# Bias sums of a projection moved from TensorE to VectorE, and one projection step written ahead of other work

## The chip, the cores and the metric

The kernel runs on one core of one Trainium2 chip. The metric is device time in microseconds (us), the median over several runs. The core has five engines that work side by side, each through its own queue: PE (matrix products, with a separate row PEld for the loads of their stationary operand), DVE (elementwise operations and reductions), ACT (activation functions and copies), POOL (here mostly issuing transfers) and SP (issuing transfers). PE writes its products to PSUM, in banks that the other engines read out.

## The reference, cut to what matters

Four images of 32 x 32 positions with 768 channels go through two layers, each of them `x = x + attention(group_norm(x))` with 12 heads of 64 channels. Layer 1 forms its q, k and v with a depthwise 3 x 3 convolution and a layer norm, and has a projection at the end:

```python
v = layer_norm(dwconv3x3(v, w_pool_v), g_v, b_v)
...
attn = softmax(qf * scale @ kf.T + rel_h + rel_w)
o = attn @ vf + ori_q
return o @ w_proj.T + b_proj
```

The layer norm of v ends with an added bias `b_v` of 64 numbers, the same for all heads. The rows of a softmax sum to one, so this bias goes through the attention unchanged and can be left out there; what it adds to the projection is one number for each output channel, `w_proj` times `b_v` repeated over the heads. The kernel works it out once, in `pbias`, together with `b_proj`.

## The kernel before, in words

Channels lie on the 128 partitions, six groups of 128 (`NC`), and the 1024 positions of an image along the free dimension, in two halves of 512 (`HALF`). A **stage** is one image in one layer; there are eight, in the order (0,0), (1,0), (0,1), (1,1), (2,0), (3,0), (2,1), (3,1) (image, layer), numbered from 0. A stage has six **items**, each a pair of heads, and the attention of an item takes 16 **steps**.

*The order of the work.* `attend` yields after each step. It writes the scores of four key tiles (L794, L796: PE) with their exponentials (L801: ACT), two steps later the four products with v (L818), and so on. A list `events` holds, for each step, the pieces of other work that are written at that point: the preparation of the next items (`Pair.plan`), group norms, and the projection of the stage before. Within a step the pieces are written in the order in which they were added to the list. PE, DVE, ACT and POOL keep the order in which the program writes their instructions; each engine takes its own instructions in that order, and waits where one needs a result that isn't there.

*PSUM.* Of the four scores written together, the first and the last use the same pair of banks (`ps_a`), the second and the third use two others (`place_b`, `place_c`), which the other work also borrows. The fourth score thus needs the first one's exponential to be done, and the other work's next bank needs the second's.

*Preparing an item of layer 1.* In its 24 steps, from -8 to 15, q, k and v are formed in turn: a product (`padded`, L131, copied out on ACT, L519), nine taps of the convolution (`taps`: DVE, L534 and L536), centring (`centre`: transposes on PE, L548, and DVE, L551 and L552), squaring (`square`: ACT, L558), the sums of squares (`squares`: DVE, L562 and L563), and `norm`: Ln and Exp on ACT (L153, L155), four small DVE operations (L157 to L160), the scaling (L574) and for v a memset (L576). At step 15 come `squares` and `norm` of v, and two taps of the next item.

*The projection* (`project`) uses seven products instead of eight for each pair of output groups, three pairs in all. `four(pair)` makes four of them, `three(pair)` the other three; every product is `m`, which accumulates over three head pairs, six matmuls (L131). Before them `sums` forms sums and differences of the attention outputs on DVE (L876). `put` adds bias and residual on DVE (L890) and, where there is one, a further term (L892), and stores; `add` is L895. In `three`, the second accumulation into a bank has to wait until L895 has read the first. The stationary operands are read from HBM in tiles `wproj_t`, two buffers, by `load`. Where the next stage is in layer 1 (stages 1, 2, 5 and 6, called `late` in the code), the six parts come at steps 9, 9 (`four`), 11 (`three`), 13, 13, 15, 17, 17, 19 of that stage; so step 15 holds `three(1)`.

*The biases.* In stage 2 only, which is (0,1), `four` computes two columns of `pbias` in each of its three calls: with the second weights tile of the pair, six matmuls with one column (L911), three head pairs for each of two output groups, then an addition on DVE (L913).

## Time and profile before

| | |
|---|---|
| median of 3 runs | 3838.24 us (3836.82 to 3839.79) |
| the profiled execution | 3838.91 us, its span 3837.1 us |
| PE busy | 3769.4 us, 98% of the span |
| DVE busy | 2468.8 us, 64% |
| ACT busy | 1792.4 us, 47% |
| L911, bias matmuls | 36 records of 250 ns, from 1465.5 to 1545.5 us |
| L895 in `three`, what PE waits for it | 7.4 us in 8 waits |

The page of a profile shows one execution. Busy times are sums over an engine's instructions with overlaps taken out; a row of the timeline gives start, length, engine, line, operation, result and inputs, the number of instructions merged into it, and in brackets how long the engine was idle before and what ended that. A float32 matmul appears as two records. Products overlap on PE: the next row can begin before the one before it ends, so the cost of a group is read from its start to the start of the next.

### The profile page before, as it was taken

How to read it: one execution, taken by the hardware profiler on the slowest of the kernel's cores; microseconds unless marked ns; L12 is line 12 of the kernel's file. 1: busy time of each engine (PE TensorE's matmuls, PEld its weight loads, DVE VectorE, ACT ScalarE, POOL GpSimd, SP SyncE). 2: the span in 40 equal slices, each digit the busy share in tenths (PEclk: the TensorE clock that was granted, in tenths of full speed). 3: DMA queues.
4: the chain of work that ended last, by engine and by line, in shares of the span. 5: the costliest groups of instructions: out<-in, count | busy, mean ns of one | idle time of the engine just before them, and what ended most of it. 6: DMA issues, size and time to landing. Idle time of an engine off the chain costs nothing.

```text
span 3837.1 us, 76049 instructions
## 1 busy us (share of the span) xinstructions
PE 3769.4 (98%) x32988; PEld 1643.0 (43%) x32988; DVE 2468.8 (64%) x3068; ACT 1792.4 (47%) x2573; POOL 478.1 (12%) x870
## 2 busy tenths in 40 slices
PE   8999999999999999999999999999999999999998
PEld 3535535533344443344535445355343444434442
DVE  2566554559678777688454564455686877867774
ACT  2455434545345553455534554254442555534552
POOL 0111100111111111111200010011111111111120
PEclk9999999999999999999999999999999999999999
DMA  4344442331431223311333222522124222142123
GB/s 151 104 123 114 135 144 90 100 80 41 123 94 48 60 55 97 120 48 48 82 113 119 56 76 60 176 61 74 43 55 142 64 58 57 48 124 61 47 57 99
DMA packets 211013, 330.61 MB, mean 86 GB/s; under 512 B 47570, under 2 KB 100562, under 8 KB 210672
## 3 DMA queue, kind: packets, MB, share of 16 engines
q1 hardware_dynamic: 122912, 212.26, 17.8%
q0 software_dynamic: 87760, 113.40, 12.4%
q8 instruction: 263, 4.31, 0.5%
q14 instruction: 78, 0.64, 0.1%
HBM read 184.62 MB, written 40.10 MB: 59 GB/s over the span
## 4 chain that ended last, share of the span: by engine, by line
PE 88%; DVE 8%; ACT 2%; issue 1%; DMA 1%; SPq 0%; DVEq 0%; POOL 0%; ACTq 0%
PE qkv L131 19%; PE s L794 16%; PE av L818 15%; PE m4m L131 5%; PE m1m L131 4%; PE m3m L131 4%; PE s L796 4%; PE p3p L131 3%; PE p4p L131 3%; PE rel L605 3%; PE p1p L131 2%; PE m L131 2%; DVE shared L536 2%; PE ln_c L548 2%; PE z L763 1%
## 5 line engine op out<-in xcount | busy, mean ns | idle before, releaser
L801 ACT ACTIVATE e<-s 128x1024 f32<-128x1024 f32 x768 | 773.5, 1024 | 415.4 <-PE s L796 386.7
L794 PE MATMUL s<-q,k 64*128 64x512 f32 x3072 | 808.2, 603 | 12.1 <-ACT e L801 11.0
L131 PE MATMUL qkv<-xn,wqkv_t 128*64 128x512 f32 x3648 | 814.3, 595 | 2.6 <-DVE gmean L323 2.6
L536 DVE SCALAR_TENSOR_TENSOR shared<-shared,sm 128x1056 f32<-128x1056 f32 x576 | 758.1, 1316 | 15.6
L796 PE MATMUL s<-bias,ones 64*128 64x512 f32 x1536 | 611.0, 789 | 0.9 <-DMA bias<-whole 0.9
L818 PE MATMUL av<-e,vt 128*64 128x512 f32 x2624 | 595.6, 596 | 0.0
L632 POOL DMA_DIRECT2D bias<-high x384 | 205.6, 555 | 2187.7 <-ACT high L621 1950.8
L131 PEld LDWEIGHTS qkv<-xn,wqkv_t 128*64 128x64 f32 x3648 | 251.3, 137 | 490.5 <-issue 484.9
L812 DVE TENSOR_TENSOR acc<-acc,e 128x1024 f32<-128x1024 f32 x294 | 360.1, 1225 | 114.3 <-ACT e L801 87.4
L794 PEld LDWEIGHTS s<-q,k 64*128 64x128 f32 x3072 | 278.8, 186 | 271.6 <-issue 209.2
L519 ACT ACTIVATE shared<-qkv,sm 128x512 f32<-128x512 f32 (+1 forms) x288 | 129.3, 502 | 501.2 <-PE qkv L131 501.2
L818 PEld LDWEIGHTS av<-e,vt 128*64 128x64 f32 x2624 | 180.7, 137 | 350.5 <-issue 316.4
L796 PEld LDWEIGHTS s<-bias,ones 64*128 64x128 f32 x1536 | 148.5, 187 | 184.7 <-issue 182.9
L632 POOL DMA_DIRECT2D bias<-whole x384 | 207.2, 572 | 51.6 <-DVE whole L622 44.8
L810 DVE TENSOR_TENSOR acc<-e 128x1024 f32<-128x1024 f32 x49 | 60.0, 1225 | 214.6 <-ACT e L801 204.5
L731 ACT COPY weighed<-av 128x512 f32<-128x512 f32 x96 | 56.4, 587 | 278.5 <-PE av L818 264.9
L551 DVE TENSOR_REDUCE mean<-ln_c 128x8 f32<-128x512 f32 x144 | 98.5, 684 | 117.1 <-PE ln_c L548 117.1
L605 PEld LDWEIGHTS rel<-q,rel 64*32 64x32 f32 x6144 | 112.0, 106 | 78.3 <-issue 73.5
L737 POOL DMA_DIRECT2D z<-weighed x47 | 27.2, 579 | 885.7 <-ACT weighed L731 480.5
L562 DVE TENSOR_REDUCE lnv<-shared 128x16 f32<-128x1024 f32 x72 | 87.5, 1216 | 69.4 <-ACT shared L558 69.4
L605 PE MATMUL rel<-q_t,rel 64*32 64x32 f32 x6144 | 123.6, 195 | 2.2 <-issue 2.2
L605 PE MATMUL rel<-q,rel 64*32 64x32 f32 x6144 | 122.7, 195 | 1.8 <-issue 1.8
(158 smaller groups left out, 4398.8 us busy)
## 6 DMA issues: line engine op xcount, KB each, us to landing
bias<-high POOLq DMA_DIRECT2D x384, 128.0 KB, 2.9
bias<-whole POOLq DMA_DIRECT2D x384, 128.0 KB, 3.1
wqkv_t<-in_wqkv SPq DMA_DIRECT2D x78, 384.0 KB, 3.3
wqkv_t<-mixed SPq DMA_DIRECT2D x66, 384.0 KB, 3.1
wproj_t<-mixed SPq DMA_DIRECT2D x48, 384.0 KB, 3.3
wqkv_t<-in_wqkv SPq DMA_DIRECT2D x66, 192.0 KB, 2.5
xn<-in_x SPq DMA_DIRECT2D x24, 512.0 KB, 8.5
x<-in_x SPq DMA_DIRECT2D x48, 256.0 KB, 3.4
```

What stands on the lines that cost most here:

```text
L131: nc.tensor.matmul(ps[lo : lo + D], a[:, lo : lo + D], b, start=start, stop=stop, **kw)
L519: nc.scalar.activation(self.pad[s][:, rows, there : there + src.shape[2]], src, AF.Identity, bias=col(self.column(s)))
L536: nc.vector.scalar_tensor_tensor(y, window, tap, y, ALU.mult, ALU.add)
L551: nc.vector.tensor_reduce(of, heads, AX.X, ALU.add)
L562: nc.vector.tensor_reduce(v, squared.rearrange("p (a d) -> p a d", d=D), AX.X, ALU.add)
L605: nc.tensor.matmul(ps[lo : lo + S, k * S : (k + 1) * S].rearrange("p (b c) -> p b c", b=2), rel[rows, 2 * self.layer + i, first : first + ...
L632: nc.gpsimd.dma_start(sets, some.unsqueeze(1).to_broadcast([D // 2, 2, QC]))
L794: nc.tensor.matmul(ps[:, j, :], k[rows, keys], q[rows, cols], start=True, stop=False)
L796: nc.tensor.matmul(ps[:, j, :], ones[rows, keys], bias[c][rows, kt // 2, :], start=False, stop=True,)
L801: nc.scalar.activation(e, ps, AF.Exp)
L812: nc.vector.tensor_tensor(acc, acc, e, ALU.add)
L818: nc.tensor.matmul(av[j * D : (j + 1) * D, :], pair.vt[:, kt, j * D : (j + 1) * D], e[:, j, :], start=(kt == 0), stop=(kt == NKT - 1),)
```

## The change

The biases of layer 1's projection are summed over the three head pairs first: one reduction on DVE adds the three 128 x 128 weight blocks of each output group, into a free part of the tile that holds the attention sums (`extra(11)`), and PE multiplies the sums with the bias column, two matmuls where there were six.

Secondly `at` gets a flag `ahead`, with which a piece is put at the front of its step's list. It is set for the projection's part at step 15 of the `late` stages, so that `three(1)` is written before `squares`, `norm` and the taps of that step. This applies in four stages, the biases in one.

```diff
             if layer and b == 0:
 
                 ps = small_bank("pbias")
-                for i, at in ((0, 3), (1, 2)):
-                    for n in range(3):
-                        w_sum = weights[4 * pair + 1][:, 3 * (at % 2) + n, :]
-                        nc.tensor.matmul(ps[:, i : i + 1], w_sum, col(LN + 5), start=(n == 0), stop=(n == 2))
+                w_sum = extra(11)[:, : 2 * P].rearrange("p (a c) -> p a c", a=2)
+                both = weights[4 * pair + 1].rearrange("p (a n) c -> p a c n", n=3)
+                nc.vector.tensor_reduce(w_sum, both, AX.X, ALU.add)
+                for i in range(2):
+                    nc.tensor.matmul(ps[:, i : i + 1], w_sum[:, 1 - i, :], col(LN + 5), start=True, stop=True)
                 some = slice(2 * pair, 2 * pair + 2)
                 nc.vector.tensor_tensor(pbias[:, some], ps[:, 0:2], sm[:, BIAS[1] + 18 :][:, some], ALU.add)
...
-    def at(step, piece):
-        events.setdefault(step, []).append(piece)
+    def at(step, piece, ahead=False):
+        pieces = events.setdefault(step, [])
+        pieces.insert(0 if ahead else len(pieces), piece)
...
         for r, n in zip((9, 11, 13, 15, 17, 19) if late else (7, 9, 11, 13, 14, 15), (2, 1) * 3):
             for _ in range(n):
-                at(first + r, lambda products=products: next(products))
+
+                at(first + r, lambda products=products: next(products), late and r == 15)
```

## The prediction

> **What bounds the kernel now.** I read the page's first part, then the waits, then the timeline of the stretches that the change touches.

> ```profile
> span 3837.1 us, 76049 instructions
> PE 3769.4 (98%) x32988; PEld 1643.0 (43%) x32988; DVE 2468.8 (64%) x3068; ACT 1792.4 (47%) x2573; POOL 478.1 (12%) x870
> ```

> PE is busy 98% of the span, and the chain that ended last is 88% PE. So a microsecond of PE work removed, or of PE idling added, moves the end by about one; DVE time counts only where PE waits for it. The list of waits holds two rows that matter (total us, times, longest):

> ```profile
> PE s L794 <- ACT e L801: 11.0, 8, 1.8
> PE p1p L131 <- DVE os_sums L895: 7.4, 8, 1.6
> ```

> The second row is what the moved piece can save. The timeline shows it four times at 1.57 to 1.58 us (PE at 1030.7, 1534.2, 2927.6, 3427.9), always in `three(1)` of step 15; the other four are 0.27 us in `three(2)`, which the change leaves alone. The timeline of PE, then of DVE (start, length, engine, line, operation, count, idle before):

> ```profile
> 1529.90 2.75 PE L131 MATMUL p<-q,wproj_t 128*64 128x512 f32 x12
> 1534.22 2.80 PE L131 MATMUL p1p<-q,wproj_t 128*64 128x512 f32 x12 [1.58 <-DVE os_sums L895]
> ```

> ```profile
> 1524.22 1.22 DVE L562 TENSOR_REDUCE lnv<-shared 128x16 f32<-128x1024 f32 x1 [2.50 <-ACT shared L558]
> 1532.24 1.32 DVE L536 SCALAR_TENSOR_TENSOR shared<-shared,sm 128x1056 f32<-128x1056 f32 x1
> 1533.48 0.68 DVE L895 TENSOR_TENSOR os_sums<-os_sums,p1p 128x512 f32<-128x512 f32 x1
> ```

> The add L895, which lets PE accumulate further into the bank, stands behind squares, norm and two taps, while DVE also idled 2.5 and 3.14 us among them.

> The biases: PE first, then DVE, around the first and second of the three places.

> ```profile
> 1462.82 2.80 PE L131 MATMUL p4p<-os_sums,wproj_t 128*64 128x512 f32 x12
> 1465.54 1.50 PE L911 MATMUL pbias<-sm,wproj_t 128*128 128x1 f32 x12
> 1466.97 2.79 PE L131 MATMUL p3p<-os_sums,wproj_t 128*64 128x512 f32 x12
> ```

> ```profile
> 1463.60 2.67 DVE L536 SCALAR_TENSOR_TENSOR shared<-shared,sm 128x1056 f32<-128x1056 f32 x2
> 1466.18 1.89 DVE L876 TENSOR_TENSOR q<-q 128x512 f32<-128x512 f32 x3
> 1467.99 0.15 DVE L913 TENSOR_TENSOR pbias<-pbias,sm 128x2 f32<-128x2 f32 x1
> ...
> 1508.62 2.67 DVE L536 SCALAR_TENSOR_TENSOR shared<-shared,sm 128x1056 f32<-128x1056 f32 x2
> 1511.21 0.15 DVE L913 TENSOR_TENSOR pbias<-pbias,sm 128x2 f32<-128x2 f32 x1
> ```

> Today PE does not wait for DVE here: it has its sums at 1466.97, and DVE comes to the addition only at 1467.99. DVE is behind PE at the first two places.

> [...] L895 above waits its turn. [...] 512 elements take 0.684 us (L551) and 1024 take 1.216 (L562), 1.04 ns for each more. [...]

> **The change, part by part.**

> *Biases, PE work.* 12 passes take 1.43 us (1465.54 to 1466.97), 0.119 each. Two matmuls instead of six are 4 passes, 0.48 us: 0.95 saved, three times 2.85, if nothing waits.

> *Biases, the reduction.* It reads 768 elements: 0.684 + 256 x 1.04 ns = 0.95 us. Its innermost step is 128 floats[...]. Bound from above by the only strided pair at hand: ACT's permuted copy takes 1.281 us (L488) against 0.778 (L487) for 512 elements, 0.98 ns more each; 768 x 0.98 = 0.75, so 1.70. Below 0.95 the row of L551 gives no reason to go. I take 0.95 and keep 1.70 for the range.

> *Biases, the new wait.* The weight load of the bias matmul now needs the reduction, and everything on PE is queued behind it. After DVE's end PE starts some 0.06 us later (1533.48 + 0.68 to 1534.22), plus 0.19 for this weight load (L911's LDWEIGHTS)[...]: 0.25.
> - Pair 0: DVE reaches the reduction at 1467.99; end 1468.94; bias matmul 1469.19; p3p 1469.67 instead of 1466.97: **2.70 lost**.
> - Pair 1: DVE 1511.21, end 1512.16, matmul 1512.41, p3p 1512.89 instead of 1509.79: **3.10 lost**. DVE is fed by PE's work between the two places, so the second loss is not covered by the first.
> - Pair 2: worked out below, since the move decides it.

> The weights are no new DMA wait: the second tile of pair 2 is issued at 1537.06 and these loads take 3.3 us to land. `w_sum` lies in the last, unused twelfth of a tile that is held anyway.

> *The move.* `three(1)` issues 18 matmuls, five DVE operations, five weight and input loads and two stores. The pieces that it passes (squares, norm of V, two taps) have nothing on PE, SP or POOL, and on ACT only Ln and Exp, of which `three` has none. So PE, ACT, SP and POOL keep their order; only DVE's five operations go ahead of ten others. In stage (0, 1), times of before:
> - p1p's first product ends 1530.07; L895 follows at once, so p1p continues at 1529.90 + 2.57 = 1532.47: 1.75 earlier, the wait and its restart.
> - It ends 1535.22. DVE's put: L890 1535.29, L892 1536.08. The squares start only now, 1536.69, instead of 1524.22; L563 at 1537.94.
> - **What is late next:** Ln and Exp of this norm precede the four exponentials of the next scores in ACT's queue. Before they ran at 1528.3, ten us ahead of need. Now Ln runs at 1538.14. The first and fourth scores share one bank (`ps_a`), so the fourth waits for the first exponential.

> The trace has this chain already, eight times; one is:

> ```profile
> 1157.35 0.22 ACT L153 ACTIVATE ln_ln<-lnv 128x16 f32<-128x16 f32 x1 [2.74 <-DVE lnv L563]
> ...
> 1158.78 1.13 PE L794 MATMUL s<-q,k 64*128 64x512 f32 x4 [1.34 <-ACT e L801]
> ```

> From Ln to the fourth score 1.43 us, and 1.30 more to what follows. So the fourth score starts at 1539.57 and p4p at 1540.87 instead of 1541.50: **0.63 gained of 1.75**, in each of four stages. Bounds: 1.75 if ACT is not late; minus 0.3 if the chain is 0.9 us slower.

> *Pair 2.* DVE comes out later: Exp ends 1538.61, four small operations to 1539.47, norm to 1540.75, three taps to 1544.69 (before, DVE idled 5.99 us here). Reduction to 1545.64, matmul 1545.89, p3p 1546.37, instead of 1545.65: **0.72 lost**, and the 0.63 is contained in it. In the other three stages DVE is next wanted at 1546.2, so its lateness is covered by 1.5 us. V's norm, ready 1540.75, is first read by the product at 1553.4.

> **Sum.** 2.70 + 3.10 + 0.72 - 3 x 0.63 = **+4.6 us**. Against the profiled run's 3838.91 (span 3837.1 and 1.8 around it) 3843.5; that run lies 0.7 above the median of 3838.24, so the median becomes 3842.8, 0.12% more.

> **The rivals.**
> - *Nothing waits*: the move keeps its 1.75 four times and the biases their 2.85: -9.85, 3828.4. For it: the PE time is truly removed. Against: DVE's clock readings above, 2.5 and 2.9 us behind PE before the reduction is added. It also needs DVE's order to differ from the written one. 0.04.
> - *ACT's hold costs nothing*: the three other stages gain 1.75 each, pair 2 stays where DVE puts it: 6.5 - 5.25 = +1.3, 3839.5. Against: the eight waits on the exponential. 0.08.
> - *The strided reduction, slower than before by more than the bound*: the three reductions in stage (0, 1) are all on the path, so each us over 0.95 counts three times. At 1.70 the sum is +6.8 (3845.1), at 2.3 us, three times ACT's excess, +8.7 (3846.9). It passes the bound from 1.98 us. 0.18.
> - The forecast, with the reduction between 0.95 and 1.70: 0.70.

> **How the numbers follow.** A measurement of this kernel can tell about 0.2%, 7.7 us, from no change: 3830.6 to 3845.9. Forecast and second rival lie inside, the first below, the third above: faster 0.04, same 0.78, slower 0.18. The forecast's own range is 3841 to 3845.5. For 8 in 10 the range reaches down to 3838.5 (the second rival) and up to 3847.5 (the reduction at 2.3).

> **What would show it.** Right: PE waits for the reduction some 3.6, 4 and 2.3 us at the three bias matmuls; L895's four waits of 1.58 are gone; four waits of about 1.3 us of the fourth score on the exponential have come, PE's first list row going from 8 to 12 times. Wrong: no PE idling before the bias matmuls, a reduction far from 0.95, or exponentials that start with their scores after `three(1)`.

## The result, and the profile after

The changed kernel takes 3850.34 us (median of 7 runs, 3846.48 to 3851.88) against 3838.24 for the kernel before: a ratio of 1.0031, 95% interval 1.0022 to 1.0039. It is 12 us slower. The forecast was 4.6 us slower, with a range that ended at 3847.5.

The first part of the page of the changed kernel, for its profiled execution of 3850.34 us:

```profile
span 3848.5 us, 76002 instructions
PE 3771.7 (98%) x32964; PEld 1639.3 (43%) x32964; DVE 2472.7 (64%) x3071; ACT 1791.5 (47%) x2573; POOL 477.8 (12%) x870
```

PE has 24 records less, as the edit says, and yet 2.3 us more of busy time. Fewer instructions with more busy time is the first sign that some of them took longer than before. The list of PE's waits (total us, times, longest):

```profile
PE s L794 <- ACT e L801: 15.2, 13, 1.8
PE pbias L912 <- DVE os_sums L910: 9.4, 3, 3.9
...
PE p1p L131 <- DVE os_sums L895: 1.1, 4, 0.3
```

The waits moved as forecast. Of L895's eight waits the four long ones are gone; the exponential has five waits more, four of them of 0.86 us in the four late stages (the fifth, of 0.77 us at 1840.9, lies outside them); and a new row has come, the bias matmul (now L912) waiting for the reduction (L910) at all three places. The first place on the timeline, PE and DVE, and then from the kernel before the row of PE that follows its p3p:

```profile
1463.04 2.79 PE L131 MATMUL p4p<-os_sums,wproj_t 128*64 128x512 f32 x12
1469.26 0.61 PE L912 MATMUL pbias<-sm,os_sums 128*128 128x1 f32 x4 [3.43 <-DVE os_sums L910]
1469.80 4.49 PE L131 MATMUL p3p<-os_sums,wproj_t 128*64 128x512 f32 x12
1474.12 2.74 PE L131 MATMUL p4p<-q,wproj_t 128*64 128x512 f32 x12
```

```profile
1466.38 1.89 DVE L876 TENSOR_TENSOR q<-q 128x512 f32<-128x512 f32 x3
1468.18 1.03 DVE L910 TENSOR_REDUCE os_sums<-wproj_t 128x256 f32<-128x768 f32 x1
```

```profile
1469.60 2.75 PE L131 MATMUL p4p<-q,wproj_t 128*64 128x512 f32 x12
```

PE idles 3.43 us for the reduction, which was foreseen. What was not: p3p, the same twelve records as before, then takes 4.32 us to the next row (1469.80 to 1474.12) instead of 2.63 (1466.97 to 1469.60). The table by stretches (length, PE, PEld, DVE, ACT and POOL busy with their instructions, the granted PE clock, the share of DMA, GB/s) says why:

```profile
1466.70:1470.10 3.40, 0.84 (x6) 0.72 (x8) 2.67 (x5) 0.23 (x1) 0.00 (x0) 1.00 0.00 0
1470.12:1473.51 3.39, 3.39 (x10) 0.96 (x8) 0.00 (x0) 0.00 (x0) 0.00 (x0) 0.50 0.00 0
1473.55:1477.00 3.45, 3.45 (x18) 1.15 (x16) 0.77 (x2) 0.00 (x0) 0.00 (x0) 1.00 0.37 114
```

From 1470.11 to 1473.53 us, for 3.41 us, PE runs at half its clock, and then at the full one again. In the 3.4 us ahead of that PE was busy for only 0.84.

The stretch from the first p4p to the second is 6.78 us at each place in the kernel before. In the changed kernel it is 11.08, 11.51 and 9.70 us, which splits as follows.

| place | p3p starts late by | p3p slower by | sum |
|---|---|---|---|
| pair 0 | 2.61 | 1.69 | 4.30 |
| pair 1 | 3.03 | 1.70 | 4.73 |
| pair 2 | 1.28 | 1.64 | 2.92 |
| all | 6.92 | 5.03 | 11.95 |

The move gives back 0.67 us in each of four stages, 2.68. The touched places together come to 11.95 - 2.68 = +9.3 us; the other 2.8 of the 12.1 lie elsewhere (see the last experiment).

### The profile page after: what moved, and what is told of

It is laid out like the page before. It is cut to its first block, busy times and chain, and to the rows that moved or that the text cites. A ratio compares the mean times of both kernels' runs of the same rounds, so it can differ in the third digit from the quotient of the medians.

```text
span 3848.5 us, 76002 instructions
## 1 busy us (share of the span) xinstructions
PE 3771.7 (98%) x32964; PEld 1639.3 (43%) x32964; DVE 2472.7 (64%) x3071; ACT 1791.5 (47%) x2573; POOL 477.8 (12%) x870
## 4 chain that ended last, share of the span: by engine, by line
PE 87%; DVE 9%; ACT 2%; issue 1%; DMA 1%; SPq 0%; DVEq 0%; POOL 0%; ACTq 0%
PE qkv L131 18%; PE av L818 15%; PE s L794 15%; PE m4m L131 5%; PE m1m L131 4%; PE m3m L131 4%; PE s L796 4%; PE p3p L131 3%; PE rel L605 3%; PE p1p L131 3%; PE p4p L131 3%; DVE shared L536 2%; PE m L131 2%; PE ln_c L548 1%; PE z L763 1%; PE p L131 1%
## 5 line engine op out<-in xcount | busy, mean ns | idle before, releaser
L801 ACT ACTIVATE e<-s 128x1024 f32<-128x1024 f32 x768 | 772.0, 1024 | 376.5 <-PE s L796 348.4
L794 PE MATMUL s<-q,k 64*128 64x512 f32 x3072 | 807.7, 602 | 16.4 <-ACT e L801 15.2
L131 PE MATMUL qkv<-xn,wqkv_t 128*64 128x512 f32 x3648 | 814.3, 595 | 2.6 <-DVE gmean L323 2.6
L536 DVE SCALAR_TENSOR_TENSOR shared<-shared,sm 128x1056 f32<-128x1056 f32 x576 | 758.3, 1316 | 15.7
L131 PEld LDWEIGHTS qkv<-xn,wqkv_t 128*64 128x64 f32 x3648 | 251.3, 137 | 490.5 <-issue 485.7
L794 PEld LDWEIGHTS s<-q,k 64*128 64x128 f32 x3072 | 277.7, 186 | 278.1 <-issue 207.9
L551 DVE TENSOR_REDUCE mean<-ln_c 128x8 f32<-128x512 f32 x144 | 98.6, 685 | 117.0 <-PE ln_c L548 117.0
L562 DVE TENSOR_REDUCE lnv<-shared 128x16 f32<-128x1024 f32 x72 | 87.5, 1216 | 59.4 <-ACT shared L558 59.4
```

Of the source, the lines that this page charges most:

```text
L131: nc.tensor.matmul(ps[lo : lo + D], a[:, lo : lo + D], b, start=start, stop=stop, **kw)
L536: nc.vector.scalar_tensor_tensor(y, window, tap, y, ALU.mult, ALU.add)
L551: nc.vector.tensor_reduce(of, heads, AX.X, ALU.add)
L562: nc.vector.tensor_reduce(v, squared.rearrange("p (a d) -> p a d", d=D), AX.X, ALU.add)
L794: nc.tensor.matmul(ps[:, j, :], k[rows, keys], q[rows, cols], start=True, stop=False)
L801: nc.scalar.activation(e, ps, AF.Exp)
```

## The experiments

The theory: PE's idling costs more than its length, because the clock is halved for a while after it. Rivals: the move costs, through DVE's late norm and taps; or the reduction's own time on DVE costs.

**The move alone** (`e1_move_alone`): the kernel before with only the second edit.

> The kernel before with the second edit alone: the projection's part at step 15 is written ahead of squares, norm and taps, the biases are left as they were. Theory (the cost lies in PE's idling before the bias matmuls and in the PE clock after it): four waits of 1.58 us on L895 go, four of about 0.86 us on the exponential come, 0.66 us gained in each of four stages, 2.6 us in all: 3835.6 us, and no stretch of lower PE clock beyond those of before. Rival (the move costs, because DVE's norm and taps come out late and something later waits for them): 3840 us or more.

Measured: 3835.78 us (13 runs) against 3838.23, ratio 0.9994 (0.9985 to 1.0002); not told apart from no change by the interval, but the median lies where the theory put it, and not where the rival did. Its list of waits:

```profile
PE s L794 <- ACT e L801: 14.3, 12, 1.8
...
PE p1p L131 <- DVE os_sums L895: 1.1, 4, 0.3
```

Twelve waits instead of eight, as the prediction said of the move. Its profile has no half clock at the touched places (the clock granted over its span is 0.999, against 0.997 in the changed kernel's). So the move is not what costs.

**The biases alone** (`e2_biases_alone`): the kernel before with only the first edit.

> The kernel before with the first edit alone: weights summed over heads by DVE, two bias matmuls where there were six, the order of step 15 as before. Theory: PE idles 3.4 and 3.9 us before the first two bias matmuls and not at the third, where DVE is free in time; 2.7 + 3.1 - 0.95 = 4.9 us, and each of the two idles is followed by some 3.4 us at half the PE clock, 1.7 us each: +8.3, 3846.5 us. Rival (an idle costs its own length and no more): +4.9, 3843.1 us, PE clock 1.0 after both.

Measured: 3847.4 us (10 runs), ratio 1.0023 (1.0013 to 1.0032), +9.2. The rival's +4.9 lies at the very edge of the interval (1.0013), so the time alone hardly excludes it, though all ten times (3845.51 and more) are above its 3843.1; the clock, which it had at 1.0, does. The timeline of PE at the two places, and one stretch at the first:

```profile
1470.43 1.02 PE L912 MATMUL pbias<-sm,os_sums 128*128 128x1 f32 x4 [3.45 <-DVE os_sums L910]
1471.38 5.39 PE L131 MATMUL p3p<-os_sums,wproj_t 128*64 128x512 f32 x12
1476.55 2.98 PE L131 MATMUL p4p<-q,wproj_t 128*64 128x512 f32 x12
...
1519.47 1.02 PE L912 MATMUL pbias<-sm,os_sums 128*128 128x1 f32 x4 [3.85 <-DVE os_sums L910]
1520.42 4.96 PE L131 MATMUL p3p<-os_sums,wproj_t 128*64 128x512 f32 x12
1525.21 2.74 PE L131 MATMUL p4p<-q,wproj_t 128*64 128x512 f32 x12
```

```profile
1470.21:1477.01 6.80, 6.58 (x18) 2.62 (x20) 0.46 (x3) 0.00 (x0) 0.00 (x0) 0.50 0.00 0
```

The third place has no wait, since DVE is not made late by the move. At the first two the half clock lasts twice as long here, 6.83 us, through the bias matmuls and nearly all of p3p: p3p alone takes 5.17 and 4.79 us to the next row. The loss after an idle is thus not a constant; the last section has what the traces show of it.

**The wait filled** (`e3_wait_filled`): the changed kernel, with PE kept busy while it waits.

```diff
+                for _ in range((8, 9, 5)[pair]):
+                    nc.tensor.matmul(ps[:, 2:512], ident, cst[:, :510], start=True, stop=True)
                 for i in range(2):
                     nc.tensor.matmul(ps[:, i : i + 1], w_sum[:, 1 - i, :], col(LN + 5), start=True, stop=True)
```

> The changed kernel with matmuls of no use (identity times constants, into unused columns of the bias bank) put on PE ahead of the bias matmuls: 8, 9 and 5 of them at the three places, 0.43 us each, about as long as PE idled there (3.4, 3.9, 2.1 us). PE reaches the product after the biases no earlier than in the changed kernel. Theory (idling lowers the clock): no half clock after the biases, the product p3p takes 2.6 us instead of 4.3, 5.1 us less than the changed kernel: 3845.2 us. Rival (the missing time has another cause than idling, DVE's lateness or the form of the bias matmuls): as the changed kernel, 3850 us or more.

Measured: 3851.67 us (5 runs), ratio 1.0035 (1.0022 to 1.0049). By its time alone the expectation (3845.2) failed, and the rival looks right. The timeline shows that the experiment was mis-sized:

```profile
1465.99 7.11 PE L912 MATMUL pbias<-cst 128*128 128x510 f32 x16
1472.93 0.50 PE L914 MATMUL pbias<-sm,os_sums 128*128 128x1 f32 x4
1473.36 2.80 PE L131 MATMUL p3p<-os_sums,wproj_t 128*64 128x512 f32 x12
1475.99 2.75 PE L131 MATMUL p4p<-q,wproj_t 128*64 128x512 f32 x12
```

Eight such matmuls took 6.94 us and not 3.4: one costs 0.87. I had taken 0.43 from L131's rows (twelve records in 2.6 us), where each matmul has only 64 stationary columns and the records start in pairs, 0.006 us apart. So p3p starts 5.95, 6.80 and 3.38 us late at the three places, 16.1 in all; less the move's 2.7 that is +13.4, and +13.4 was measured. Nothing is left for a lower clock, and p3p takes 2.63 us, its old length, although DVE is as late and the bias matmuls have the same form as in the changed kernel.

**The wait filled, as it turned out** (`e4_wait_shortened`): the same with `(4, 5, 1)`. It was meant to leave 1.7 us of idling each time.

> As the kernel with filled waits, but with 4, 5 and 1 matmuls of no use, so that PE still idles about 1.7 us at each of the three places. Theory (only idles of about 1.9 us and more halve the clock; the kernel before shows 1.76 without and 1.96 with it): PE clock 1.0 after all three, p3p 2.6 us, 3845.2 us, as with the waits filled. Rival (every idle of over a us lowers the clock, or for a time in proportion): about 3847 to 3850 us, with p3p well above 2.6 us.

With 0.87 us each, four and five matmuls fill the first two waits wholly; at the third 1.06 us of idling is left.

```profile
1465.18 3.69 PE L912 MATMUL pbias<-cst 128*128 128x510 f32 x8
1468.76 0.61 PE L914 MATMUL pbias<-sm,os_sums 128*128 128x1 f32 x4
1469.29 2.79 PE L131 MATMUL p3p<-os_sums,wproj_t 128*64 128x512 f32 x12
1471.92 2.74 PE L131 MATMUL p4p<-q,wproj_t 128*64 128x512 f32 x12
```

Measured: 3842.44 us (21 runs), ratio 1.0012 (1.0005 to 1.0018). This is the run that decides: p3p starts 2.69, 3.38 and 1.29 us late, as late as in the changed kernel or later, DVE has the same work, PE has *more*, and the kernel is 7.9 us faster by the medians (7.2 by the later median of the changed kernel, below); the intervals of the ratios don't touch. What it lacks is most of the idling, and with it the half clock: p3p takes 2.63 us at all three places, which is 5.0 of the difference. The rest isn't explained by it. Its +4.2 us is nearly what the prediction had for the whole change.

**Half of the wait left** (`e8_wait_halved`): `(2, 2, 1)`.

> The changed kernel with 2, 2 and 1 matmuls of no use ahead of the bias matmuls; such a full-width one took 0.87 us in the runs before this, twice what was reckoned, so the kernel with 4, 5 and 1 of them had filled the first two waits wholly. Here PE still idles about 1.7, 2.1 and 1.1 us, and comes to the product after the biases no earlier than in the changed kernel. Theory (an idle of about 2 us or more can halve the clock, a shorter one does not): no half clock at the first and third place, at the second perhaps; 3842.5 us, as with 4, 5 and 1, up to 3846. Rival (any idle of over a us lowers the clock for a time): half clock at all three, 3847 to 3850 us.

```profile
1469.04 0.61 PE L914 MATMUL pbias<-sm,os_sums 128*128 128x1 f32 x4 [1.54 <-DVE os_sums L910]
1469.57 4.49 PE L131 MATMUL p3p<-os_sums,wproj_t 128*64 128x512 f32 x12
...
1554.76 0.61 PE L914 MATMUL pbias<-sm,os_sums 128*128 128x1 f32 x4 [1.05 <-DVE os_sums L910]
1555.30 2.80 PE L131 MATMUL p3p<-os_sums,wproj_t 128*64 128x512 f32 x12
```

Measured: 3844.67 us (15 runs), ratio 1.0018 (1.0011 to 1.0026). Idles of 1.54 and 1.95 us were both followed by the half clock in the profile (0.70 and 0.74 in the mean of the 3 us from the bias matmuls on), the one of 1.05 was not (1.00). So the limit of about 2 us was wrong at the first place: 1.58 to 1.76 us passed unpunished in the kernel before, 1.54 did not here. Whether the one-column bias matmuls that follow, another 0.53 us up to p3p, have a part in it was not shown; no run tests that alone.

**The bias matmuls later** (`e5_matmul_later`): the changed kernel with the reduction where it was, and what needs it moved two products further on (the lines with + stood ahead of the first m before).

```diff
             m(b2, pair, 1, lambda n: extra(n + 3), range(n_first))
...
             m(b1, pair, 2, x11, more=True)
+            if layer and b == 0:
+                ps = small_bank("pbias")
+                for i in range(2):
+                    nc.tensor.matmul(ps[:, i : i + 1], w_sum[:, 1 - i, :], col(LN + 5), start=True, stop=True)
+                some = slice(2 * pair, 2 * pair + 2)
+                nc.vector.tensor_tensor(pbias[:, some], ps[:, 0:2], sm[:, BIAS[1] + 18 :][:, some], ALU.add)
```

> The changed kernel with the two bias matmuls and their addition written two products later (behind p3p and the second p4p), the reduction left where it is: by then DVE has long finished it. Theory (the loss is PE's idling for the reduction and the clock after it): no wait at the bias matmuls, no half clock there, 0.95 us of PE work less three times and 0.66 us less in four stages: -5.5, 3832.8 us. Rival (the reduction's 1 us on DVE in the stage of the biases is itself what costs): 3838 us or more.

Measured: 3834.33 us (13 runs), ratio 0.9991 (0.9983 to 1.0). PE no longer stops:

```profile
1465.19 2.74 PE L131 MATMUL p3p<-os_sums,wproj_t 128*64 128x512 f32 x12
1467.77 2.74 PE L131 MATMUL p4p<-q,wproj_t 128*64 128x512 f32 x12
1470.44 0.61 PE L916 MATMUL pbias<-sm,os_sums 128*128 128x1 f32 x4
```

The same reduction at the same place in DVE's order now holds up nothing: from the first p4p to the second p3p each place takes 8.41 us against 9.35 in the kernel before, 0.94 of the 0.95 that the edit removes from PE. So the third theory, that its time on DVE costs, falls. The median gained 3.6 us and not 5.5, and its interval just reaches no change; the profile has the 5.5 at the touched places, so what is missing lies outside them.

**The move, behind the norm** (`e6_move_behind_norm`): the kernel before, with `three(1)` third in its step, behind squares and norm and ahead of the taps.

```diff
-    def at(step, piece):
-        events.setdefault(step, []).append(piece)
+    def at(step, piece, place=None):
+        pieces = events.setdefault(step, [])
+        assert place is None or len(pieces) == 3
+        pieces.insert(len(pieces) if place is None else place, piece)
...
-                at(first + r, lambda products=products: next(products))
+                at(first + r, lambda products=products: next(products), 2 if late and r == 15 else None)
```

> The kernel before with three(1) of step 15 written behind squares and norm of V, but ahead of the two taps; biases as before. Theory (in the changed kernel Ln, late on ACT, holds the exponentials): L895 starts at norm's end, some 0.9 us before PE needs it, Ln runs as early as before, so neither wait is left: 1.75 us gained in each of four stages, -7.0, 3831.2 us. Rival (some other wait takes its place, as with the move to the front): as the move alone, 3835.8 us.

Measured: 3831.41 us (21 runs), ratio 0.9982 (0.9976 to 0.9989), -6.6 where -7.0 was expected. ACT, then PE:

```profile
1525.96 0.21 ACT L153 ACTIVATE ln_ln<-lnv 128x16 f32<-128x16 f32 x1
```

```profile
1536.18 1.03 PE L794 MATMUL s<-q,k 64*128 64x512 f32 x4
```

Ln runs ten us ahead of need again, and the fourth score starts without a wait. Against the move to the front (`e1_move_alone`) that is 1.0 us more in each stage: what the move gained too little there went to ACT's queue.

**Both mended** (`e7_both_mended`): the last two edits together.

> Both mended edits together: three(1) behind norm and ahead of the taps, the reduction with its matmuls two products later. Theory: the gains add, -2.85 and -7.0, 3828.4 us, better than the kernel before and the changed one. Rival (PE has no more to give there, the gains overlap): 3831 us or more.

Measured: 3829.2 us (20 runs), ratio 0.9978 (0.9971 to 0.9984), 9 us better than before and 21 better than the changed kernel. The gains nearly add.

**The changed kernel again** (`e9_changed_again`).

> The changed kernel once more, for a second look at the three stretches of half clock and more timed executions. By its first profile the half clock cost 1.69 us three times, 5.1 us, while the kernel with the first two waits filled was 7.9 us faster by the medians. If the stretches vary in length from one execution to the next (as in the profile of the biases alone, where p3p took 5.2 us and p4p was slowed too), this profile shows at least one place that costs 2.5 us or more, and the times spread over some 5 us; median 3848 to 3851 us. If each place costs 1.7 us in every execution, the median should fall to about 3847.5.

Measured: 3849.63 us (10 runs, 3846.95 to 3852.47), ratio 1.0028 (1.0019 to 1.0038). The three places cost the same as in the first profile, to 0.1 us; neither branch of the expectation holds as a whole. The touched places give +9.3, the medians +11.3 to +12.1. In both profiles of the changed kernel the missing 2 to 3 us lie in stretches that the change does not touch: against the profile of before, the same rows come 0.9 and 1.1 us later by 880 us, and another 1.3 and 1.5 between 1960 and 2780. The other runs' profiles show 1.4 later to 0.5 earlier in the first of these and 1.2 later to 0.2 earlier in the second, with PE at its full clock, so most of it looks like the scatter of executions; whether a part belongs to the change stays open.

## Why the prediction was wrong

*The step that failed* stands in its first paragraph: "a microsecond of PE work removed, or of PE idling added, moves the end by about one". For idling at the bias matmuls that did not hold: p3p came 6.9 us late in all, as forecast, and then lost 5.0 us more at half clock. The sum had no term for what an idle does to the products behind it, and its range was made of the strided reduction, which turned out harmless. That it is the idling and not the lateness, `e4_wait_shortened` shows: p3p as late, all but one short idle filled, full clock, +4.2. For work removed the rule came out nearer: `e7_both_mended` is 2.2 us faster than `e6_move_behind_norm`, for 2.85 us of PE work less. The remaining 2 to 3 us of the measured 12.1 (11.3 in the second series) are not accounted for.

*It could be read in the profile of before.* The timeline of PE near that kernel's end has it, after an idle of 1.99 us, and the table by stretches its clock:

```profile
3782.03 0.19 PE L1032 MATMUL good<-good,cst 128*1 128x1 f32 x2 [1.99 <-DVE good L1030]
3782.46 4.49 PE L131 MATMUL p1p<-os_sums,wproj_t 128*64 128x512 f32 x12 [0.24 <-DVE bad L1034]
```

```profile
3783.00:3786.00 3.00, 3.00 (x12) 0.88 (x10) 0.00 (x0) 0.00 (x0) 0.00 (x0) 0.56 0.42 132
```

Twelve records in 4.30 us to the next row (at 3786.76), at a clock of 0.56: the same picture as p3p above.

*What held, step by step.*
- The reduction: 1.025 us measured, 0.95 forecast; the strided step added at most 0.08, not the 0.75 of the upper bound, which was an estimate from ACT's copies (1.281 us permuted, 0.778 not). The slower rival named the wrong mechanism, and its 2.3 us, "three times ACT's excess", leaves out the 0.95 that its bound of 1.70 includes. With it the reduction would have been 3.20 us and the sum +11.4, close to the measured time by luck.
- The new waits: p3p late by 2.61, 3.03 and 1.28 against 2.70, 3.10 and 1.35 (0.72 and the 0.63 that it contained). The bias matmul starts 0.05 us after the reduction's end, not 0.25; against that, the reduction is 0.08 slower and the bias matmuls take 0.54 instead of 0.48. That these errors nearly cancel is luck.
- The move: 0.67 us a stage against 0.63. In the changed kernel, ACT and then PE:

```profile
1547.37 0.22 ACT L153 ACTIVATE ln_ln<-lnv 128x16 f32<-128x16 f32 x1 [9.67 <-DVE lnv L563]
```

```profile
1548.79 1.13 PE L794 MATMUL s<-q,k 64*128 64x512 f32 x4 [0.86 <-ACT e L801]
```

From Ln to the fourth score 1.42 us, as in the chain that the prediction took for its model; the wait that shows is 0.86 and not 1.3. (Seven of the eight waits of before have this chain; at 3717.7 us ACT is held by copies.)
- *Nothing waits* fell at once, by the 9.4 us of waits. *ACT's hold costs nothing* fell by `e1_move_alone` and, the other way round, by `e6_move_behind_norm`, whose profile has the full 1.8 us a stage once the hold is gone.

*What the runs show of the slow clock:* it is the half (0.50), and the slow stretches last 3.41 us, or twice that. They came after idles down to 1.54 us, in windows of that length in which PE was busy for up to 0.45 of the time, once 0.55 (the last section).

## What to carry to other kernels

A wait on the engine that bounds a kernel is not priced by its length alone: look up what the same engine's clock does after waits of that length elsewhere in the same profile, and price the slow stretch too (here about 1.7 us for each 3.41 us of half clock). Before moving work off the bounding engine, read where the other engine's queue stands at that moment; if it is behind, put the consumer later, behind work that is ready (here two products further, which turned +12 us into -4). When a piece is put ahead of others, put it ahead of what may be late, and leave in front what another in-order queue waits for (here Ln in ACT's queue, which came late and cost a wait of 0.86 us on PE in each late stage).
